# Experts' second layers by seven products, with combinations of tokens on GpSimd and the halves of images reordered

## Chip, cores and metric

The kernel runs on one core of a Trainium2 chip. The metric is the time of one execution on the device in microseconds (us), as the median of several runs. PE is the matmul engine, DVE the vector engine, ACT the scalar engine, POOL is GpSimd, SP issues most of the transfers. SBUF is the memory on the chip that holds the kernel's tiles; a bank is a tile of PSUM, into which PE writes its products.

## The reference

The program is two attention layers on 8 images of 256 channels and 32 x 32 pixels, with a mixture of experts at the end. The change concerns the experts alone. Every expert handles every token, and the gate weighs the results:

```python
def _L1_ffn_ref(x, Wr, br, W1, b1, g1, be1, m1, v1, W2, b2, g2, be2, m2, v2, Wo, bo):
    feat = jnp.mean(x, axis=0)                       # over all images
    w = jax.nn.softmax(feat @ Wr + br, axis=-1)      # the gates
    h = jnp.einsum('bfd,edh->bfeh', x, W1) + b1
    h = jax.nn.relu(_bn(h, g1, be1, m1, v1))
    h = jnp.einsum('bfeh,ehk->bfek', h, W2) + b2
    h = jax.nn.relu(_bn(h, g2, be2, m2, v2))
    y = jnp.einsum('bfeh,ehd->bfed', h, Wo) + bo
    return jnp.einsum('bfed,fe->bfd', y, w)
```

`feat` is a mean over all eight images, so no gate is known before the last image's attention has ended. First and second layers need no gate; the third does, since the kernel weighs its input and sums the experts on PE.

## The kernel before

The work comes in 128 units: 8 images, 2 halves of 512 pixels, 8 experts. Each unit has a first, a second and a third layer, each one product of a 256 x 256 weight with 256 x 512 data. First and third layers use **seven products** for eight (`products` and `sums`, Winograd's form of Strassen's scheme): the weights are combined once (`weights`), the tokens once per input (`combined`), and `sums` puts the result together on DVE. Second layers use eight plain products (`half`). Second layers that are done before the gates are known are stored in DRAM and fetched back later. `f` is a small model of the engines' times by which background work is placed; it emits the instructions.

```python
    def load(tile_i):
        b, half = divmod(tile_i, 2)
        f.finish(lambda: ended[0] > b)
        h = xs[tile_i] = T(work, [P, 2, 512], "hn", bufs=3)
        f.sp.dma_start(h, hn[b][:, :, half * 512 : half * 512 + 512])
...
    def bank():
        return T(psum, [P, 512], "bank", bufs=4)

    def half(dst, wt, e, src, s, c, m):

        ps = bank()
        for k in range(2):
            f.pe.matmul(ps, lhsT=wt[:, k, m * P : (m + 1) * P], rhs=src[:, k, :], start=k == 0, stop=k == 1)
        f.act.activation(dst[:, m, :], ps, AF.Relu, bias=col(c, e, m), scale=col(s, e, m))

    def where(i):
        tile_i, e = divmod(i, NE)
        b, half = divmod(tile_i, 2)
        return tile_i, e, b, slice(half * 512, half * 512 + 512)
...
    def blocks(w):

        return w[:, 0, :P], w[:, 1, :P], w[:, 1, P:]

    def weights(w, tag, pool):
        s = T(pool, [P, 4, P], tag)
        a11, a12, a22 = blocks(w)
        f.pool.tensor_tensor(s[:, 0, :], w[:, 0, P:], a22, ALU.add)
        f.pool.tensor_tensor(s[:, 1, :], s[:, 0, :], a11, ALU.subtract)
        f.pool.tensor_tensor(s[:, 2, :], a11, w[:, 0, P:], ALU.subtract)
        f.pool.tensor_tensor(s[:, 3, :], a12, s[:, 1, :], ALU.subtract)
        return s

    def combined(h, tag, pool=work):

        t = T(pool, [P, 4, C], tag, bufs=2)
        f.ve.tensor_tensor(t[:, 0:2, :], h[:, :, C:], h[:, 0, :].rearrange("p (n q) -> p n q", n=2), ALU.subtract)
        f.ve.tensor_tensor(t[:, 2, :], h[:, 1, C:], t[:, 0, :], ALU.subtract)
        f.ve.tensor_tensor(t[:, 3, :], h[:, 1, :C], t[:, 2, :], ALU.subtract)
        return t
...
    def products(banks, w, s, h, t, begin, end):

        a11, a12, a22 = blocks(w)
        for bank, place, lhs, rhs in (
            (1, 0, a11, h[:, 0, :C]),
            (0, 0, a12, h[:, 1, :C]),
            (0, 1, s[:, 1, :], t[:, 2, :]),
            (2, 0, s[:, 0, :], t[:, 0, :]),
            (2, 1, s[:, 2, :], t[:, 1, :]),
            (3, 0, s[:, 3, :], h[:, 1, C:]),
            (3, 1, a22, t[:, 3, :]),
        ):
            f.pe.matmul(
                banks[bank][:, place * C : place * C + C],
                lhsT=lhs,
                rhs=rhs,
                start=begin and (end or place == 0),
                stop=end and (begin or place == 1 or bank == 1),
            )

    def sums(banks):

        c = T(work, [P, 4, C], "c", bufs=2)
        u = T(work, [P, 2, C], "u", bufs=2)
        p26, p57, p34 = (banks[i].rearrange("p (u q) -> p u q", u=2) for i in (0, 2, 3))
        p1 = T(work, [P, 1, C], "p1c", bufs=2)
        f.act.activation(p1[:, 0, :], banks[1][:, :C], AF.Copy)
        f.ve.tensor_tensor(c[:, 0::2, :], p1.to_broadcast([P, 2, C]), p26, ALU.add)
        f.ve.tensor_tensor(u, c[:, 2:3, :].to_broadcast([P, 2, C]), p57, ALU.add)
        f.ve.tensor_tensor(c[:, 3, :], u[:, 1, :], p57[:, 0, :], ALU.add)
        f.ve.tensor_tensor(c[:, 1:3, :], u, p34, ALU.add)
        return c.rearrange("p (m n) q -> p m (n q)", m=2)

    def first7(i):
        tile_i, e, _, _ = where(i)
        if tile_i not in ts:
            ts[tile_i] = combined(xs[tile_i], "t1")
        h = h1s[i] = T(work, [P, 2, 512], "h1", bufs=2)
        banks = [bank() for _ in range(4)]
        products(banks, w1[e], s1[e], xs[tile_i], ts[tile_i], True, True)
        c = sums(banks)
        for m in range(2):
            f.act.activation(h[:, m, :], c[:, m, :], AF.Relu, bias=col(1, e, m), scale=col(0, e, m))
        loaded(i)
        if e == NE - 2 and tile_i + 1 in xs:
            ts[tile_i + 1] = combined(xs[tile_i + 1], "t1")

    def second(i, staged):
        _, e, _, _ = where(i)
        h, src = T(work, [P, 2, 512], "h2", bufs=5), h1s.pop(i)
        for m in range(2):
            half(h, w2[e], e, src, 2, 3, m)
            yield
        if staged:
            f.sp.dma_start(h2d[i], h)
        else:
            h2s[i] = h

    def fetch(i):
        if i not in h2s:
            h = h2s[i] = T(work, [P, 2, 512], "h2", bufs=5)
            f.sp.dma_start(h, h2d[i])
...
    f.step((PACE2, PACE2))
    while not gated and n2 < NSTAGED:
        ahead()
    f.finish(lambda: gated)
    early.close()
    wp3 = ctx.enter_context(tc.tile_pool(name="w3", bufs=1, side="right"))

    gb = T(wp3, [P, NE, HW], "gates")
    f.split(gb, *(512 * i for i in range(1, 2 * NE)))
    for part in range(2):
        sl = slice(part * 512, part * 512 + 512)
        for e in range(NE):
            f.sp.dma_start(gb[:, e, sl], gtd[e : e + 1, sl].to_broadcast([P, 512]))
    psum_y = ctx.enter_context(tc.tile_pool(name="psum_y", bufs=1, space=PSUM, side="right"))

    def weigh(i):
        _, e, _, sl = where(i)
        h = h2s[i]
        f.ve.tensor_tensor(h, h, gb[:, e : e + 1, sl].to_broadcast([P, 2, 512]), ALU.mult)
        h2s[i] = h, combined(h, "t3", wp3)

    def third(i):
        tile_i, e, b, sl = where(i)
        if e == 0:
            y = [T(psum_y, [P, 512], f"y{m}") for m in range(4)]
            t = T(work, [P, 2, 512], "t2")
            f.sp.dma_start(t, t2[b][:, :, sl])
            f.ve.tensor_tensor(t, t, gated[0][:, :, sl], ALU.add)
            ys[tile_i] = y, t
        y, t = ys[tile_i]
        products(y, wo[e], s3[e], *h2s.pop(i), e == 0, e == NE - 1)
        if e == NE - 1:
            f.ve.tensor_tensor(t, sums(y), t, ALU.add)
            f.sp.dma_start(out[b].rearrange("(k p) n -> p k n", p=P)[:, :, sl], t)
            ys.pop(tile_i)

    s3 = {}
    for i in range(NE):
        s3[i] = weights(wo[i], f"s3e{i}", wp3)

    def thirds(count):
        nonlocal n3
        for _ in range(count):
            if n3 < n2:
                if n3 + 2 < n2:
                    fetch(n3 + 2)
                if n3 + 1 < n2:
                    weigh(n3 + 1)
                third(n3)
                n3 += 1

    for i in range(2):
        ahead()
        fetch(i)
    weigh(0)
    while n3 < total:
        many = n2 > n3 + 2
        if n2 < n1 - 1 or n1 == total and n2 < total:
            halves = second(n2, n2 > n3 + 2)
            next(halves)
            thirds(1)
            for _ in halves:
                pass
            n2 += 1
            if many:
                thirds(1)
        else:
            thirds(1 + many)
        if n1 < total:
            first7(n1)
            n1 += 1
```

Of the kernel before, what the change touches and what calls it, by code (L numbers as in the profile page):

```python
# [10 lines left out]
AF = mybir.ActivationFunctionType  # L11
ALU = mybir.AluOpType
# [22 lines left out]
AHEAD = {"DVE": 4.0, "ACT": 2.0, "POOL": 1.0, "SP": 10.0}  # L35
NEAR = {"DVE": 1.5, "ACT": 2.0, "POOL": 1.0, "SP": 10.0}
BUFS = {"sm": 2, "sx": 1}
PACE2 = 8.0
NBOUND = 64
NSTAGED = 64  # L40
# [1947 lines left out]
def experts(tc, kit, nb, t2, hn, h2d, w1c, w2_d, wo_d, bnvec, bo_d, gate_d, wrc, consts8, gtd, out, f, outer, ended, early):  # L1988
# [8 lines left out]



    with ExitStack() as ctx:  # L2000
        l1, shared = outer
        wp = ctx.enter_context(tc.tile_pool(name="w2", bufs=1))
# [4 lines left out]
        xs = {}  # L2007

        def load(tile_i):
            b, half = divmod(tile_i, 2)  # L2010
            f.finish(lambda: ended[0] > b)
            h = xs[tile_i] = T(work, [P, 2, 512], "hn", bufs=3)
            f.sp.dma_start(h, hn[b][:, :, half * 512 : half * 512 + 512])

        w1, w2, wo = ([T(wp, [P, 2, C], f"{name}{e}") for e in range(NE)] for name in ("w1e", "w2e", "wo"))
# [73 lines left out]
        def col(what, e, m):  # L2089
            return bnvec[:, what * 2 * NE + 2 * e + m : what * 2 * NE + 2 * e + m + 1]  # L2090

        h1s, h2s, ys, ts = {}, {}, {}, {}

        def bank():
            return T(psum, [P, 512], "bank", bufs=4)
# [7 lines left out]

        def where(i):
            tile_i, e = divmod(i, NE)
            b, half = divmod(tile_i, 2)
            return tile_i, e, b, slice(half * 512, half * 512 + 512)

        def loaded(i):
# [5 lines left out]

        def first(i):
            tile_i, e, _, _ = where(i)
            h = h1s[i] = T(work, [P, 2, 512], "h1", bufs=2)
            for m in range(2):
                half(h, w1[e], e, xs[tile_i], 0, 1, m)  # L2120
            loaded(i)
# [11 lines left out]
            f.pool.tensor_tensor(s[:, 3, :], a12, s[:, 1, :], ALU.subtract)  # L2133
            return s

        def combined(h, tag, pool=work):

            t = T(pool, [P, 4, C], tag, bufs=2)
            f.ve.tensor_tensor(t[:, 0:2, :], h[:, :, C:], h[:, 0, :].rearrange("p (n q) -> p n q", n=2), ALU.subtract)
            f.ve.tensor_tensor(t[:, 2, :], h[:, 1, C:], t[:, 0, :], ALU.subtract)  # L2140
            f.ve.tensor_tensor(t[:, 3, :], h[:, 1, :C], t[:, 2, :], ALU.subtract)
            return t

        def products(banks, w, s, h, t, begin, end):
# [17 lines that stand above are left out]
                    stop=end and (begin or place == 1 or bank == 1),  # L2162
                )

        def sums(banks):

            c = T(work, [P, 4, C], "c", bufs=2)
            u = T(work, [P, 2, C], "u", bufs=2)
            p26, p57, p34 = (banks[i].rearrange("p (u q) -> p u q", u=2) for i in (0, 2, 3))
            p1 = T(work, [P, 1, C], "p1c", bufs=2)  # L2170
            f.act.activation(p1[:, 0, :], banks[1][:, :C], AF.Copy)
            f.ve.tensor_tensor(c[:, 0::2, :], p1.to_broadcast([P, 2, C]), p26, ALU.add)
            f.ve.tensor_tensor(u, c[:, 2:3, :].to_broadcast([P, 2, C]), p57, ALU.add)
            f.ve.tensor_tensor(c[:, 3, :], u[:, 1, :], p57[:, 0, :], ALU.add)
            f.ve.tensor_tensor(c[:, 1:3, :], u, p34, ALU.add)
            return c.rearrange("p (m n) q -> p m (n q)", m=2)

        def first7(i):
            tile_i, e, _, _ = where(i)
            if tile_i not in ts:  # L2180
                ts[tile_i] = combined(xs[tile_i], "t1")
            h = h1s[i] = T(work, [P, 2, 512], "h1", bufs=2)
            banks = [bank() for _ in range(4)]
            products(banks, w1[e], s1[e], xs[tile_i], ts[tile_i], True, True)
            c = sums(banks)
            for m in range(2):
                f.act.activation(h[:, m, :], c[:, m, :], AF.Relu, bias=col(1, e, m), scale=col(0, e, m))
            loaded(i)
            if e == NE - 2 and tile_i + 1 in xs:
                ts[tile_i + 1] = combined(xs[tile_i + 1], "t1")  # L2190

        def second(i, staged):
            _, e, _, _ = where(i)
            h, src = T(work, [P, 2, 512], "h2", bufs=5), h1s.pop(i)
            for m in range(2):
                half(h, w2[e], e, src, 2, 3, m)
                yield
            if staged:
                f.sp.dma_start(h2d[i], h)
            else:  # L2200
                h2s[i] = h

        def fetch(i):
            if i not in h2s:
                h = h2s[i] = T(work, [P, 2, 512], "h2", bufs=5)
                f.sp.dma_start(h, h2d[i])

        total = 2 * nb * NE
        f.spawn(gates(), 7)
        n1 = n2 = n3 = 0  # L2210
        s1 = {e: weights(w1[e], f"s1e{e}", wp) for e in range(NE)}

        def ahead():
            nonlocal n1, n2

            (first if n1 < 3 else first7)(n1)
            if n1 == 0:
                ts[0] = combined(xs[0], "t1")
            n1 += 1
            f.step((PACE2, PACE2))  # L2220
            if n1 > 1:
                for _ in second(n2, True):
                    pass
                n2 += 1
                f.step((PACE2, PACE2))

        f.step((PACE2, PACE2))
        while not gated and n2 < NSTAGED:
            ahead()
        f.finish(lambda: gated)  # L2230
        early.close()
        wp3 = ctx.enter_context(tc.tile_pool(name="w3", bufs=1, side="right"))

        gb = T(wp3, [P, NE, HW], "gates")
        f.split(gb, *(512 * i for i in range(1, 2 * NE)))
        for part in range(2):
            sl = slice(part * 512, part * 512 + 512)
            for e in range(NE):
                f.sp.dma_start(gb[:, e, sl], gtd[e : e + 1, sl].to_broadcast([P, 512]))
        psum_y = ctx.enter_context(tc.tile_pool(name="psum_y", bufs=1, space=PSUM, side="right"))  # L2240

        def weigh(i):
            _, e, _, sl = where(i)
            h = h2s[i]
            f.ve.tensor_tensor(h, h, gb[:, e : e + 1, sl].to_broadcast([P, 2, 512]), ALU.mult)
            h2s[i] = h, combined(h, "t3", wp3)

        def third(i):
            tile_i, e, b, sl = where(i)
            if e == 0:  # L2250
                y = [T(psum_y, [P, 512], f"y{m}") for m in range(4)]
                t = T(work, [P, 2, 512], "t2")
                f.sp.dma_start(t, t2[b][:, :, sl])
                f.ve.tensor_tensor(t, t, gated[0][:, :, sl], ALU.add)
                ys[tile_i] = y, t
            y, t = ys[tile_i]
            products(y, wo[e], s3[e], *h2s.pop(i), e == 0, e == NE - 1)
            if e == NE - 1:
                f.ve.tensor_tensor(t, sums(y), t, ALU.add)
                f.sp.dma_start(out[b].rearrange("(k p) n -> p k n", p=P)[:, :, sl], t)  # L2260
                ys.pop(tile_i)

        s3 = {}
        for i in range(NE):
            s3[i] = weights(wo[i], f"s3e{i}", wp3)

        def thirds(count):
            nonlocal n3
            for _ in range(count):
                if n3 < n2:  # L2270
                    if n3 + 2 < n2:
                        fetch(n3 + 2)
                    if n3 + 1 < n2:
                        weigh(n3 + 1)
                    third(n3)
                    n3 += 1

        for i in range(2):
            ahead()
            fetch(i)  # L2280
        weigh(0)
        while n3 < total:
            many = n2 > n3 + 2
            if n2 < n1 - 1 or n1 == total and n2 < total:
                halves = second(n2, n2 > n3 + 2)
                next(halves)
                thirds(1)
                for _ in halves:
                    pass
                n2 += 1  # L2290
                if many:
                    thirds(1)
            else:
                thirds(1 + many)
            if n1 < total:
                first7(n1)
                n1 += 1


@with_exitstack  # L2300
# [179 lines left out]
```

## Time and profile before

| | before |
|---|---|
| median of the runs, us | 3362.33 (3358.39 to 3362.58) |
| busy PE / DVE / ACT / POOL, us | 3175.6 / 2311.2 / 1688.4 / 511.1 |
| first matmul of the experts | 2002.02 us, after 8.55 us of waiting |
| first third layer | 2289.97 us, after 10.97 us of waiting |
| last two matmul records of the third layers start | 3347.21 us |

Lines of the timeline give start, duration, engine, instruction and what ended an idle time before it in brackets; durations of matmuls overlap in the pipeline, so lengths here are differences of starts. The transfers issued by SP at the moment the gates are known:

```profile
2267.42 11.79 SPq L668 DMA_DIRECT2D gates<-gtd  x16
...
2280.27 3.27 SPq L668 DMA_DIRECT2D h<-h  x5
```

Sixteen broadcasts of gates occupy the queue until 2279.2 us. The stored second layer that the first third layer needs is fetched behind them. The second view is the group of the weighing on DVE (busy time, mean ns of one, idle time before it):

```profile
L668 DVE TENSOR_TENSOR h<-h,gates 128x1024 f32<-128x1024 f32 x127 | 154.7, 1218 | 7.1 <-ACT h L668 7.1
```

### The profile page before, as it was taken

Reading aid. Unit: us, or ns where it says so; the run is one execution under the profiler, and the core shown is the slowest. Engines: PE = TensorE matmul, PEld = TensorE weight load, DVE = VectorE, ACT = ScalarE, POOL = GpSimd, SP = SyncE. Lnnn points to the kernel's source line nnn. Section 1 sums busy time; section 2 is a strip of 40 time slices with the busy share of each in tenths; the row PEclk is TensorE's granted clock in tenths of the full one; section 3 lists DMA queues with packets and bytes.
Section 4 is the critical chain, followed back from the end, with each engine's and each line's share of the span. In section 5 each row is a group of like instructions: output and inputs, shape, how many; then the busy total and the mean of one; then the engine's idle time right before and its main releaser. Section 6 shows DMA issues by size and latency. Waiting matters only on the chain.

```text
span 3365.0 us, 40262 instructions
## 1 busy us (share of the span) xinstructions
PE 3175.6 (94%) x15352; PEld 1801.8 (54%) x15352; DVE 2311.2 (69%) x3972; ACT 1688.4 (50%) x2225; POOL 511.1 (15%) x644
## 2 busy tenths in 40 slices
PE   8687899899899999899899989998999999999997
PEld 4332244344345345345344346766777777777775
DVE  5687787886886886887874446346776666666665
ACT  4476676576576666666666533342223333333332
POOL 2211414213214114214211120010000000000000
PEclk9798999999999999999999999999999999999999
DMA  2357646656646655556556565125441100000000
GB/s 74 83 120 166 130 98 155 130 103 150 131 102 142 141 134 122 121 137 126 115 124 139 117 184 184 51 93 189 145 155 65 36 19 19 19 19 19 19 13 20
DMA packets 106363, 345.88 MB, mean 103 GB/s; under 512 B 13025, under 2 KB 38377, under 8 KB 82929
## 3 DMA queue, kind: packets, MB, share of 16 engines
q0 software_dynamic: 28608, 179.85, 27.8%
q1 hardware_dynamic: 74192, 161.40, 13.9%
q8 instruction: 123, 2.02, 0.2%
q10 hardware_dynamic: 3360, 1.97, 0.2%
q14 instruction: 80, 0.65, 0.1%
HBM read 104.59 MB, written 73.44 MB: 53 GB/s over the span
## 4 chain that ended last, share of the span: by engine, by line
PE 64%; DMA 2%; ACT 2%; issue 2%; DVE 1%; POOL 1%; SPq 0%; ACTq 0%; POOLq 0%; DVEq 0%
PE bank L668 23%; PE sm L668 13%; PE y L668 12%; PE sc L668 6%; PE sx L668 6%; PE pv L668 5%; ACT pt L668 2%; DMA pt<-pt 1%; DMA hn<-hn 0%; DMA feat<-hn 0%; POOL rstd L668 0%; DVE rec L668 0%; DMA gates<-gtd 0%; DMA w1e<-w1c 0%; POOL pt L668 0%
## 5 line engine op out<-in xcount | busy, mean ns | idle before, releaser
L668 ACT ACTIVATE pt<-sc 128x2048 f32<-128x2048 f32 (+1 forms) x384 | 719.9, 1875 | 326.1 <-PE sc L668 278.4
L668 DVE SCALAR_TENSOR_TENSOR acc<-p,vec,acc 128x225 f32<-128x225 f32 (+7 forms) x928 | 527.8, 576 | 29.4 <-ACT acc L668 4.9
L668 PE MATMUL sc<-q,kn 32*128 32x512 f32 (+1 forms) x3072 | 445.8, 650 | 95.8 <-ACT pt L668 94.4
L668 DVE TENSOR_TENSOR pt<-pt,pt 128x1024 f32<-128x1024 f32 x320 | 387.4, 1254 | 141.0 <-DMA pt<-pt 136.1
L668 PE MATMUL bank<-h,w2e 128*128 128x512 f32 x1024 | 480.1, 595 | 0.0
L668 PE MATMUL pv<-pt,vt 128*32 128x512 f32 (+1 forms) x3072 | 418.0, 617 | 0.0
L668 ACT ACTIVATE h<-bank,bnvec 128x512 f32<-128x512 f32 x262 | 201.3, 769 | 385.7 <-PE bank L668 374.0
L668 ACT ACTIVATE h<-c,bnvec 128x512 f32<-128x512 f32 x250 | 189.9, 807 | 385.7 <-DVE c L668 385.7
L668 DVE TENSOR_TENSOR c<-p1c,bank 128x512 f32<-128x512 f32 x125 | 85.9, 687 | 350.9 <-PE bank L668 349.9
L668 POOL DMA_DIRECT2D pt<-pt x192 | 173.9, 907 | 779.0 <-ACT pt L668 628.4
L668 PEld LDWEIGHTS bank<-h,w2e 128*128 128x128 f32 x1024 | 195.2, 191 | 149.8 <-issue 134.9
L668 PEld LDWEIGHTS sc<-q,kn 32*128 32x128 f32 (+1 forms) x3072 | 116.3, 178 | 284.8 <-ACT pt L668 185.5
L668 PEld LDWEIGHTS pv<-pt,vt 128*32 128x32 f32 (+1 forms) x3072 | 60.7, 108 | 301.8 <-issue 290.1
L668 POOL TENSOR_TENSOR rstd<-rstd,mhalf 128x4 f32<-128x4 f32 (+2 forms) x88 | 107.9, 1227 | 675.6 <-DVE rstd L668 616.4
L668 PE MATMUL y<-t,s3e 128*128 128x256 f32 x768 | 188.0, 381 | 0.0
L668 PE MATMUL bank<-t,s1e 128*128 128x256 f32 x750 | 183.2, 380 | 0.2 <-ACT h L668 0.2
L668 PE MATMUL sm<-y,t 128*128 128x256 f32 x752 | 180.9, 385 | 0.0
L668 DVE TENSOR_TENSOR h<-h,gates 128x1024 f32<-128x1024 f32 x128 | 156.0, 1218 | 19.3 <-issue 12.2
L668 PEld LDWEIGHTS sm<-y,t 128*128 128x128 f32 x752 | 137.8, 190 | 56.5 <-issue 35.1
L668 ACT ACTIVATE p<-sm 128x512 f32<-128x512 f32 (+1 forms) x151 | 88.4, 585 | 145.2 <-PE sm L668 122.0
L668 PEld LDWEIGHTS y<-t,s3e 128*128 128x128 f32 x768 | 146.8, 191 | 20.2
L668 PEld LDWEIGHTS bank<-t,s1e 128*128 128x128 f32 x750 | 143.1, 191 | 20.2 <-ACT h L668 0.6
(303 smaller groups left out, 4689.4 us busy)
## 6 DMA issues: line engine op xcount, KB each, us to landing
pt<-pt POOLq DMA_DIRECT2D x160, 1024.0 KB, 7.4
h<-h SPq DMA_DIRECT2D x88, 512.0 KB, 3.8
xi<-in_x_dram SPq DMA_DIRECT2D x16, 512.0 KB, 6.7
t<-t SPq DMA_DIRECT2D x8, 1024.0 KB, 9.3
res<-t SPq DMA_DIRECT2D x32, 256.0 KB, 4.1
t<-res SPq DMA_DIRECT2D x32, 256.0 KB, 4.9
hn<-res SPq DMA_DIRECT2D x32, 256.0 KB, 2.9
hn<-hn SPq DMA_DIRECT2D x16, 512.0 KB, 5.5
```

Source lines behind the costliest of these rows:

```text
L668: ins = fn(*args, **kwargs)
```

## The change

Intent: less matmul work after the gates. PE is the bound there, GpSimd is idle, and PE also waits once at the gates. The change has these parts:

- second layers go by seven products too, once the gates are known (`strassen = bool(s3)`): weights' sums `s2` and tokens' combinations `tm` on GpSimd;
- most combinations for third layers move to GpSimd as well (`weighed(f.pool)`), except that in the first passes (rounds of the loop at the end of the cut), where two third layers go with one second (`many`), one of the two stays on DVE;
- the two activations of a seven-product layer are held back until the next layer's copy (`late`, `flush`);
- tiles are in the order of halves: the first half of all eight images, then the second. Eight gate rows are held for sixteen, and each is replaced when its half is done;
- at the gates, three stored layers are fetched before the broadcasts, and a first layer stands before the first third layer;
- the start of the experts may take up to eight steps of background work for one;
- the residual of a half image is fetched and added nearer to its end.

The diff, cut to its core:

```diff
-            b, half = divmod(tile_i, 2)
+            half, b = divmod(tile_i, nb)
...
-        def combined(h, tag, pool=work):
+        def combined(h, tag, pool=work, eng=f.pool):
...
+        def layer7(e, w, s, src, t, first, tag, bufs, then):
+            banks = [bank() for _ in range(4)]
+            products(banks, w[e], s[e], src, t, True, True)
+            h = sums(banks, tag, bufs)
+
+            def relu():
+                for m in range(2):
+                    f.act.activation(h[:, m, :], h[:, m, :], AF.Relu, bias=col(first + 1, e, m), scale=col(first, e, m))
+                then(h)
+
+            late.append(relu)
 
         def first7(i):
...
+            strassen = bool(s3)
+            if strassen and e not in s2:
+                s2[e] = weights(w2[e], f"s2e{e}", wp3)
+
+            def then(h):
+                h1s[i] = h
+                if strassen:
+                    tms[i] = combined(h, "tm", wp3)
+
+            layer7(e, w1, s1, xs[tile_i], ts[tile_i], 0, "h1", 3, then)
...
         def second(i, staged):
...
+            if i in tms:
+                layer7(e, w2, s2, src, tms.pop(i), 2, "h2", 6, then)
             else:
-                h2s[i] = h
+                h = T(work, [P, 2, 512], "h2", bufs=6)
+                for m in range(2):
+                    half(h, w2[e], e, src, 2, 3, m)
+                then(h)
...
-        f.step((PACE2, PACE2))
+        for _ in range(NE):
+            f.step((PACE2, PACE2))
+            if max(f.ready[a.name] for a in (w1[0], xs[0])) <= f.now["PE"]:
+                break
...
         f.finish(lambda: gated)
+        for i in range(AHEAD3):
+            fetch(i)
...
-        gb = T(wp3, [P, NE, HW], "gates")
-        for part in range(2):
...
+        def spread(e, sl):
+            gb[e] = T(wp3, [P, 1, 512], f"gate{e}")
+            f.sp.dma_start(gb[e][:, 0, :], gtd[e : e + 1, sl].to_broadcast([P, 512]))
+
+        for e in range(NE):
+            spread(e, slice(0, 512))
...
+        def weighed(eng):
+            if n3 + AHEAD3 < n2:
+                fetch(n3 + AHEAD3)
+            if n3 + 1 < n2:
+                weigh(n3 + 1, eng)
...
         while n3 < total:
             many = n2 > n3 + 2
             if n2 < n1 - 1 or n1 == total and n2 < total:
-                halves = second(n2, n2 > n3 + 2)
...
+                second(n2, many)
                 n2 += 1
                 if many:
-                    thirds(1)
-            else:
-                thirds(1 + many)
+                    weighed(f.pool)
+                    thirds()
+            weighed(f.ve if many else f.pool)
             if n1 < total:
                 first7(n1)
                 n1 += 1
+            thirds()
```

## The prediction

> **What bounds the kernel now.** I read the page's engine shares and slices first, then the sums by stretch, then the timeline of the last stretch, then the waits around the moment the gates become known. The first lines to read are these:
>
> ```profile
> PE 3175.6 (94%) x15352; PEld 1801.8 (54%) x15352; DVE 2311.2 (69%) x3972; ACT 1688.4 (50%) x2225; POOL 511.1 (15%) x644
> PE   8687899899899999899899989998999999999997
> DVE  5687787886886886887874446346776666666665
> POOL 2211414213214114214211120010000000000000
> ```
>
> PE is busy 94% of the span, and from slice 28 on it never drops. The experts' part after the gates is slices 28 to 40. There GpSimd (POOL) does nothing and DVE is about 60 to 70% busy. The sums by stretch (PE, PEld, DVE, ACT, POOL) say it sharply:
>
> ```profile
> 2002.00:2280.00 278.00, 273.08 (x1026) 190.74 (x1026) 128.47 (x236) 103.92 (x175) 40.78 (x77) 0.98 0.38 130
> 2290.00:2450.00 160.00, 160.00 (x635) 122.44 (x636) 115.58 (x175) 41.35 (x64) 0.00 (x0) 0.98 0.43 150
> 2570.00:3348.00 778.00, 777.80 (x2956) 561.17 (x2954) 477.58 (x745) 266.35 (x417) 0.00 (x0) 1.00 0.06 19
> ```
>
> From 2290 to 3348 us PE has no gap. Only two things shorten that stretch: fewer matmul columns, or nothing. The timeline there shows what one unit (one expert on one half image) costs; second layer = bank<-h,w2e, first layer = bank<-hn,..., third layer = y:
>
> ```profile
> 3001.74 1.88 PE L668 MATMUL bank<-h,w2e 128*128 128x512 f32 x4
> 3003.46 1.03 PE L668 MATMUL bank<-hn,w1e 128*128 128x256 f32 x4
> ...
> 3006.48 1.88 PE L668 MATMUL bank<-h,w2e 128*128 128x512 f32 x4
> 3008.20 1.03 PE L668 MATMUL y<-h,wo 128*128 128x256 f32 x4
> ...
> 3011.22 1.88 PE L668 MATMUL bank<-h,w2e 128*128 128x512 f32 x4
> ```
>
> Durations overlap in this pipeline, so I use starts. Half a second layer takes 3003.46 - 3001.74 = 1.72 us, a whole one 3.44 us (8 matmul records of 0.43). A seven-product layer takes 3006.48 - 3003.46 = 3.02 us (14 records of 0.216). A unit is 3.44 + 3.02 + 3.02 = 9.48 us.
>
> The one large hole of PE in the experts' part is at the gates:
>
> ```profile
> 2275.40 3.60 PE L668 MATMUL bank<-h,w2e 128*128 128x512 f32 x8
> 2289.97 2.08 PE L668 MATMUL y<-h,wo 128*128 128x256 f32 x4 [10.97 <-DVE h L668]
> 2291.84 2.77 PE L668 MATMUL y<-t,s3e 128*128 128x256 f32 x6
> ```
>
> PE waits 10.97 us for the first weighing on DVE, and the ten records after it take 4.4 us of starts instead of 2.2: the clock has to come back. A smaller hole, 8.55 us, lies at 2002 us, where the first hn and weights are loaded.
>
> **What the Trainium skill says.** (1) "TensorE: Matmul & The Clock Gate", Part 1: an idle array drops to half clock and needs some microseconds of activity to return. The trace agrees: 0.52 us per 256-column record after the hole against 0.26 by its record mean, both including pipeline time, or 2.08 against 1.03 for the same four. (2) "GPSIMD Engine Reference", section 3: two-input elementwise work is about half as fast on GpSimd. Here 128x512 with two SBUF inputs takes 1.32 us on POOL (pool<-xi) and 0.69 us on DVE (t<-h); 128x256 takes 0.78 against 0.42. (3) "SBUF — State Buffer", section "Who interferes with whom": a DVE instruction with two SBUF inputs and a GpSimd instruction that reads SBUF block each other for a whole instruction; with at most one SBUF input DVE is free of it. The trace agrees: the shared stretch below has two DVE additions of 1.22 us each taking 3.33 us and two POOL additions, otherwise 0.95 us each, taking 2.95 us.
>
> ```profile
> 1285.05 3.33 DVE L668 TENSOR_TENSOR pt<-pt,pt 128x1024 f32<-128x1024 f32 x2
> 1287.37 2.95 POOL L668 TENSOR_TENSOR pool<-pool,xi 128x320 f32<-128x320 f32 x2
> ```
>
> **The change, part by part.**
>
> *Second layers on PE.* Of 1024 w2e records (8 per unit, 128 units), 194 start before 2285 us, so about 24 second layers are done when the loop starts. The unit whose first layer came just before also has no combination ready. That leaves 128 - 25 = 103 layers to switch: 103 x (3.44 - 3.02) = 43 us less on PE.
>
> *The hole at the gates.* Before, sixteen gate broadcasts of 256 KB (4 MB) take the queue from 2267.4 to 2279.2 us and the fetch of the first stored h2 stands behind them. Now three fetches go first, only eight broadcasts (2 MB) follow, and a first layer is put ahead of the first third layer. I expect 11 us of waiting and 2 us of slow clock gone: 13 us. The start at 2002 us may now run background work while the load lands; but a background matmul is only taken if its data is already there, so I count 2 of 8.55 us.
>
> *The order of halves* makes the gates of one half enough for eight images. About 22 units are done before the gates, which needs images 0 to 4 only, all ended by then. I count no time for it.
>
> *DVE.* Each switched layer adds four sums: 0.69 + 0.69 + 0.42 + 0.68 = 2.48 us, so 103 x 2.48 = +255 us. About 104 of the 128 third-layer combinations (0.69 + 2 x 0.42 = 1.54 us) go to POOL: -160 us. Net about +95 us, to some 2405 us.
>
> *POOL.* A combination costs 1.32 + 2 x 0.78 = 2.9 us; 103 for the second layer and 104 for the third give 600 us, plus 8 x 1.85 us for the weights' sums (four of 0.46 us per expert). POOL goes from 511 to about 1125 us.
>
> *ACT.* Two activations (1.54 us) become a copy (0.37) and two activations (1.6): +0.4 us x 103 = 41 us, beside the rest.
>
> **Does that fit under PE?** About 20 loop passes come first in which two third layers are done per second layer (44 of the h<-h transfers' 88 are stores, 24 of them before the loop). PE needs 4 x 3.02 = 12.1 us a pass. DVE has two sets of sums (5.0), two weighings (2.4), one combination (1.5), and on average 1.4 for the y sums, residuals and t1: 10.4 us. POOL has 5.8 us, and in the first eight passes up to 5.5 more for weights. The two-SBUF-input part of DVE (about 4.8 us) plus POOL is 10.6 us, and up to 16 in the first passes: it must be run one after the other while the sums also wait their turn on DVE. I expect here 0.9 us of PE waiting per pass, 18 us, and 8 more while the weights are made.
> In the other 84 passes PE needs 9.07 us, DVE 5.0 + 1.2 + 0.8 = 7.0, POOL 5.8. Second and first layer now stand next to each other on PE and share four banks: from the trace the first DVE sum starts 1.56 us after a layer's first matmul and the last ends 4.1 us after, while the next layer needs the last bank at 3.02 + 2.2 = 5.2 us. So banks are free in time unless DVE is late by over about 0.9 us. It is late once per eight passes, when the y sums (2.5) and the residual (1.2) come on top: about 0.8 us x 11 = 8 us. The last two units add the longer POOL combination to the end: 2 us.
>
> Sum: 3362 - 43 - 13 - 2 + 18 + 8 + 8 + 2 = 3340 us. The losses are my weakest terms, taken at the pessimistic end of a hand-drawn order of instructions; the deferred activations and the split of combinations between engines look tuned to avoid them. I halve them, 36 to about 20, and predict **3325 us**.
>
> **Rivals.** (A) *Nothing is lost*: PE stays at 100%, 3362 - 58 = 3304 us. For it: DVE and POOL sums both lie below PE in every pass. Against it: the lock above, and one set of four banks. (B) *DVE with the shared port becomes the bound* in the first 20 passes, and banks come free late in the others: 36 to 55 us lost, so 3340 to 3360 us, the change nearly cancelled. For it: the 3.33 us pair above, and 16 us of shared work in the first passes. Against it: after eight passes it falls below PE's time. (C) *The staged part before the gates gets slower*, because activations are held back behind the next layer's copy, or because loading an image that has not ended stalls the stream: +5 to 20 us. For it: each held-back activation has only some 0.4 us to spare. Against it: images 0 to 4 end long before.
>
> **Range and chances.** A gives the low end with a few us for the start, 3298; B without C gives 3355. Faster by 2% means below 3295 us, 67 us less: it needs all of A and the whole start, 6%. Slower by 2% means above 3430, for which B and C together do not suffice: 2%. Within 2%: 92%.
>
> **What would show each step.** PE records: w2e at 512 columns falls to about 200, and the new 256-column second-layer records start 0.216 us apart. The hole of 10.97 us is below 3 us. DVE is near 2405 us busy and POOL near 1125. Lost time shows as idle PE before bank or y records released by DVE sums or POOL combinations, most of it in the first 250 us after the gates and then once per eight units. POOL and DVE combinations longer than 1.32 and 0.69 us show the lock. I am wrong if PE is idle over 40 us after the gates, or if the part before them changes by over 15 us.

## The result, and the profile after

The median is **3332.22 us** (four runs, 3328.18 to 3334.62) against 3362.45 us for the kernel before in the same rounds (3358.39 to 3368.05). The ratio is 0.9908, with a 95% interval of 0.9889 to 0.9926: within 2%. Outputs are correct.

Busy time and slices of the page after:

```profile
PE 3137.4 (94%) x15970; PEld 1912.8 (57%) x15970; DVE 2472.4 (74%) x4069; ACT 1734.4 (52%) x2328; POOL 1227.3 (37%) x1300
...
PE   8687899999999999899899999999999999999997
...
DVE  5687788786887886886884555446998787787776
...
POOL 2211413213213214213211112006666776777775
```

PE has 38 us less, DVE 161 more, POOL 716 more. POOL now works from slice 28 to the end. The dip of PE's row at the gates (slice 28 before) is gone. The timeline of PE there, and SP's queue:

```profile
2273.62 3.60 PE L669 MATMUL bank<-h,w2e 128*128 128x512 f32 x8
2277.05 1.03 PE L669 MATMUL bank<-hn,w1e 128*128 128x256 f32 x4
...
2280.08 1.03 PE L669 MATMUL y<-h,wo 128*128 128x256 f32 x4
```

```profile
2265.15 2.56 SPq L669 DMA_DIRECT2D h<-h  x4
2267.81 6.37 SPq L669 DMA_DIRECT2D gate<-gtd  x8
```

No bracket: the third layer follows the first layer without a wait, and at 1.03 us for four records the clock is at full speed (2.08 before). The steady loop, 700 us later:

```profile
2974.64 1.03 PE L669 MATMUL bank<-h,w2e 128*128 128x256 f32 x4
...
2977.66 1.03 PE L669 MATMUL bank<-hn,w1e 128*128 128x256 f32 x4
...
2980.69 1.03 PE L669 MATMUL y<-h,wo 128*128 128x256 f32 x4
...
2983.71 1.03 PE L669 MATMUL bank<-h,w2e 128*128 128x256 f32 x4
```

Each layer takes 3.02 us, the unit 9.07 us instead of 9.48. So the matmuls shrank as planned. What came in exchange stands in the sums by stretch (stretch, its length, busy PE, PEld, DVE, ACT, POOL with their instructions, clock, DMA share, GB/s):

```profile
2280.20:2555.00 274.80, 261.89 (x1187) 223.80 (x1186) 246.78 (x311) 78.57 (x130) 183.51 (x174) 1.00 0.42 149
...
2555.00:3293.00 738.00, 735.58 (x3397) 644.36 (x3396) 578.98 (x819) 303.45 (x496) 526.61 (x485) 1.00 0.08 25
```

In the first 275 us after the gates PE is idle for 12.9 us, and a busy PE is not yet a full one. Counted by records (1187, of which 8 are 512 columns wide and count double, at 0.216 us) the work is 258.1 us, so 16.7 us are lost there. In the 738 us of the steady loop, 3397 x 0.216 = 733.7 us: 4.3 lost. Who was waited for in the two stretches (total us, times, longest):

```profile
PE y L669 <- POOL t L669: 8.6, 7, 1.8
PE bank L669 <- DVE h L669: 4.1, 5, 1.1
...
PE bank L669 <- DVE h L669: 2.4, 10, 0.3
```

Before, PE waited for nothing after its one hole at the gates. One pass of the first stretch shows how these waits arise:

```profile
2392.17 1.30 POOL L669 TENSOR_TENSOR tm<-h 128x512 f32<-128x512 f32 x1 [6.86 <-ACT h L669]
...
2392.84 3.39 DVE L669 TENSOR_TENSOR h<-h,gate 128x1024 f32<-128x1024 f32 x2
...
2393.55 3.27 POOL L669 TENSOR_TENSOR tm<-h,tm 128x256 f32<-128x256 f32 x2
...
2396.78 1.74 POOL L669 TENSOR_TENSOR t<-h 128x512 f32<-128x512 f32 x1
...
2398.60 1.66 POOL L669 TENSOR_TENSOR t<-h,t 128x256 f32<-128x256 f32 x2
...
2399.44 1.56 PE L669 MATMUL y<-t,s3e 128*128 128x256 f32 x6 [0.99 <-POOL t L669]
```

Two weighings on DVE (1.22 us each before) take 3.39 us, two GpSimd subtractions (0.78 us each by the prediction's row) take 3.27, and they lie in the same 4 us. GpSimd gets to the third layer's combination `t` late, and PE waits 0.99 us for it. Over the whole part after the gates, DVE's and POOL's groups:

```profile
L669 DVE TENSOR_TENSOR h<-h,gate 128x1024 f32<-128x1024 f32 x126 | 206.6, 1649 | 2.5 <-DMA h<-h 2.1 <-ACT h L669 0.5
```

```profile
L669 POOL TENSOR_TENSOR tm<-h,tm 128x256 f32<-128x256 f32 x206 | 247.6, 1202 | 16.1
```

The weighing went from 1218 to 1649 ns, the subtraction from 0.78 to 1.20 us. The sums on DVE, with one input in SBUF and one in PSUM, ran beside the same GpSimd and kept their 0.69 us (688 ns before):

```profile
L669 DVE TENSOR_TENSOR u<-h,bank 128x512 f32<-128x512 f32 x206 | 141.6, 687 | 21.7
```

On DVE only the instructions with two SBUF inputs got longer in this part. That is what the Trainium skill's "SBUF — State Buffer", "Who interferes with whom", leads one to expect of a two-input DVE instruction beside a GpSimd one that reads SBUF. Whether it is the cause is tested below.

**The balance of the profiled runs.** The span went from 3365.0 to 3332.1 us, 32.9 less. I split it at the start of the first third layer (2289.97 and 2280.08) and at the start of the last two records of the last one (3347.21 and 3313.95).

| stretch | before | after | difference |
|---|---|---|---|
| start to the first third layer | 2289.97 | 2280.08 | -9.9 |
| first third layer to the last | 1057.2 | 1033.9 | -23.4 |
| rest | 17.8 | 18.1 | +0.3 |

The first row is the hole at the gates (-11.0) and a start of the experts that came 1.1 us later (2003.16 for 2002.02; over the runs below, experiment 10 left out, this start lies between 1996.6 and 2003.7 us, so 1.1 us says nothing of the change). From that start, without the hole, both kernels take 277 us, though the changed one does one first layer more in it; why this layer is free there I did not settle. The second row is 103 switched layers x 0.41 us of PE = -42.2, that one first layer done earlier = -3.0, the slow clock after the hole = -1.9, and PE's waiting = **+24.5**: -22.6 together, with 0.8 left over. The 24.5 us come from experiment 1, which has no waiting: its 1051.6 us for this stretch less 42.2 is 1009.4 us of work, and the changed kernel took 1033.9. By place it is 16.7 in the first 275 us, 4.3 in the steady loop and 2.1 in the last two units (waits of 1.32 and 0.45 us on POOL with the pipeline's restart); the remaining 1.4 are within the accuracy of the count. The first row varies: over all profiled runs of the changed kernel and its variants without a hole the first third layer starts between 2273.6 and 2280.1 us, though the program before it is the same (but for the order of halves in experiment 5; experiment 10 is left out). Where small differences matter I therefore compare the second row and not the time.

### The profile page after: what moved, and what is told of

Same layout as the page of the kernel before. It is cut to its first block, busy times and chain, and to the rows that moved or that the text cites. A ratio compares the mean times of both kernels' runs of the same rounds, so it can differ in the third digit from the quotient of the medians.

```text
span 3332.1 us, 42942 instructions
## 1 busy us (share of the span) xinstructions
PE 3137.4 (94%) x15970; PEld 1912.8 (57%) x15970; DVE 2472.4 (74%) x4069; ACT 1734.4 (52%) x2328; POOL 1227.3 (37%) x1300
## 4 chain that ended last, share of the span: by engine, by line
PE 57%; DVE 5%; issue 3%; ACT 3%; POOL 3%; DMA 2%; SPq 0%; DVEq 0%; POOLq 0%; ACTq 0%
PE bank L669 18%; PE sm L669 13%; PE y L669 8%; PE sc L669 6%; PE sx L669 6%; PE pv L669 5%; DVE h L669 2%; ACT pt L669 2%; POOL tm L669 1%; DVE u L669 1%; DMA pt<-pt 1%; ACT h L669 1%; POOL t L669 1%; DVE t L669 1%; DVE c L669 1%
## 5 line engine op out<-in xcount | busy, mean ns | idle before, releaser
L669 ACT ACTIVATE p1c<-bank 128x256 f32<-128x256 f32 x228 | 87.2, 383 | 576.4 <-PE bank L669 576.1
L669 ACT ACTIVATE h<-h,bnvec 128x512 f32<-128x512 f32 x456 | 345.0, 805 | 50.7 <-DVE h L669 43.7
L669 DVE TENSOR_TENSOR h<-p1c,bank 128x512 f32<-128x512 f32 x228 | 155.2, 681 | 194.7 <-PE bank L669 191.2
L669 POOL TENSOR_TENSOR tm<-h,tm 128x256 f32<-128x256 f32 x206 | 247.6, 1202 | 16.1
L669 DVE TENSOR_TENSOR h<-u,bank 128x256 f32<-128x256 f32 x456 | 232.1, 550 | 7.9
L669 POOL TENSOR_TENSOR tm<-h 128x512 f32<-128x512 f32 x103 | 133.9, 1300 | 245.2 <-ACT h L669 241.2
L669 DVE TENSOR_TENSOR h<-h,gate 128x1024 f32<-128x1024 f32 x128 | 209.1, 1642 | 2.5 <-DMA h<-h 2.1
L669 PE MATMUL bank<-h,w2e 128*128 128x256 f32 (+1 forms) x612 | 198.8, 453 | 4.1 <-DVE h L669 4.1
L669 POOL TENSOR_TENSOR t<-h,t 128x256 f32<-128x256 f32 x210 | 177.4, 845 | 16.5
L669 DVE TENSOR_TENSOR u<-h,bank 128x512 f32<-128x512 f32 x228 | 156.7, 687 | 24.0
```

The lines of the kernel that those rows point to most:

```text
L669: ins = fn(*args, **kwargs)
```

## The experiments

My theory: the products give their 42 us and the hole its 13; PE gives 24.5 us back, and it does so because DVE and GpSimd hold each other up over SBUF while both work for the same PE. Rivals: that GpSimd is simply too slow or too late; that the weights' sums made in the first passes are to blame; that the new order of halves brought the gain. All edits below are against the changed kernel. "Waiting" is computed as above: the stretch from the first to the last third layer, less the work, which is 1051.6 us minus 0.41 us per switched layer. It rests on one profiled execution of each kernel; experiments 1 and 5, with the same work, agree in it (1051.62 us both). It counts more than the idle time that the profile shows, since PE is not at once at its full pace after a wait (the six records after the 0.99 us wait above took 1.56 us, six without a wait 1.46).

### 1. Full second layers

```diff
-            strassen = bool(s3)
+            strassen = False
```

> Second layers back to eight full-width records everywhere, all else of the change kept. Theory (43 us of matmul time bought, some 24 us of it given back as PE waiting after the gates): PE work rises by 103 x 0.42 = 43 us, DVE loses 255 us and GpSimd 300 us of work, so the waiting after the gates falls from 24 to about 5 us; time about 3332 + 43 - 19 = 3356 us, and against the kernel before only the hole at the gates is gained. Rival (the products bought nothing, the gain is all in the order of transfers at the gates): time stays at 3330 to 3335 us.

Measured: 3348.08 us (3343.41 to 3351.52), ratio 0.9967 (0.9946 to 0.9988). The weighing took 1220 ns again. PE over the experts' part after the gates:

```profile
2275.00:3326.00 1051.00, 1051.00 (x4049) 768.95 (x4048) 511.39 (x730) 343.00 (x532) 306.62 (x335) 1.00 0.16 56
```

PE is busy for 1051.00 of 1051.00 us: all the waiting belongs to the seven-product second layers, although 105 of the 128 third layers' combinations are still on POOL. (Some 5 us of waiting were expected to stay; so the run was 8 us faster than expected.) The switch of the second layers is worth 1051.6 - 1033.9 = 17.7 us net, of 42.2 gross.

### 2. Gates before the fetches

Sixteen broadcasts (each of the eight sent twice) ahead of the three fetches:

```diff
-        for i in range(AHEAD3):
-            fetch(i)
...
-        for e in range(NE):
-            spread(e, slice(0, 512))
+        for _ in range(2):
+            for e in range(NE):
+                spread(e, slice(0, 512))
+        for i in range(AHEAD3):
+            fetch(i)
```

> Sixteen gate broadcasts (each of the eight sent twice) ahead of the three fetches of stored second layers, as the kernel before had it; all else of the change kept. Theory (the 11 us hole was the queue: 4 MB of broadcasts in front of the fetch): a PE gap of 5 to 10 us in front of the first third layer, less than before because one first layer now stands ahead of it, and time 3338 to 3343 us. Rival (the hole closed because a first layer now stands ahead, or because GpSimd makes the weights one expert at a time): no gap over 2 us, time 3330 to 3335 us.

Measured: 3340.75 us (3338.46 to 3344.44), ratio 0.9947 (0.9928 to 0.9965), so about 8 us slower than the changed kernel. SP's queue and PE at the gates:

```profile
2260.30 11.90 SPq L669 DMA_DIRECT2D gate<-gtd  x16
```

```profile
2281.83 2.08 PE L669 MATMUL y<-h,wo 128*128 128x256 f32 x4 [6.93 <-DVE h L669]
```

The hole comes back with its slow clock. It is 6.93 us and not 10.97, and the first layer that the change put ahead of the third one would account for 3.02 of those 4 us. So the order of the transfers is shown to matter; that the first layer in front does is argued from its length, not tested.

### 3. Combinations for second layers made only twice (wrong result)

```diff
-                    tms[i] = combined(h, "tm", wp3)
+                    if len(kept) < 2:
+                        kept.append(combined(h, "tm", wp3))
+                    tms[i] = kept[i % len(kept)]
```

> Wrong result on purpose: GpSimd makes the combination of second-layer inputs only twice and every second layer uses one of the two; PE, DVE and ACT run the same instructions, GpSimd loses about 101 x 3 instructions. Theory (the waiting after the gates comes from GpSimd and DVE blocking each other and from GpSimd's own queue): DVE's weighing falls from a mean of 1649 ns to 1220 to 1350, PE waiting after the gates from 24 us to under 8, time about 3315 us. Rival (the waiting is DVE's own sums and the four shared banks): weighing as it may be, waiting stays above 18 us and time at 3326 to 3334 us.

Measured: 3311.38 us (3306.03 to 3313.51), ratio 0.985 (0.9831 to 0.9869), waiting 7.0 us; the weighing took 1233 ns. All seven-product matmuls and all sums on DVE are still there. So the 101 combinations that GpSimd no longer made cost 17.5 of the 24.5 us, and DVE's added sums alone do not. This does not yet say how: by occupying GpSimd's queue or by locking DVE.

### 4. All weights' sums before the first weighing

```diff
         for i in range(2):
             ahead()
+        for i in range(NE):
+            s3[i] = weights(wo[i], f"s3e{i}", wp3)
+            e = (n1 + i) % NE
+            s2[e] = weights(w2[e], f"s2e{e}", wp3)
         weigh(0)
```

> The sums of weights for second and third layers (16 x 4 GpSimd instructions of 0.46 us) all issued at once when the gates are known, when GpSimd is idle, instead of one expert at a time inside the first eight passes. Theory (17 of the 24 us of waiting lie in the first 275 us after the gates, about half of it because weights and combinations together overload GpSimd): 6 us less, 3326 us, and the waits of y for GpSimd in the first 100 us gone. Rival (that waiting is the lock and DVE, not the weights): 3330 to 3335 us.

Measured: 3333.57 us (3331.1 to 3339.18), ratio 0.9925 (0.9904 to 0.9945), waiting 27.4 us. No gain. In the first 100 us from the first third layer on, POOL was busy for 66.6 us in place of 79.0, and yet PE was idle for 6.0 us, in the changed kernel for 5.7; in the next 100 us, idle for 3.7 us in both. So the weights' sums are not what the first passes wait for, and of the prediction's 8 us for them at most some 2 (5.7 - 3.7) can have been there.

### 5. The old order of halves

With seven products in the second layers the old order could not be built: if the gates of both halves are held at once, the pool `w3` needs 80 KB per partition where 66.9 KB were left (no run shows it). So the order was tested with full second layers, against experiment 1: the two changes of `where` and `load` undone, sixteen gate tiles, and

```diff
-            half, b = divmod(tile_i, nb)
+            b, half = divmod(tile_i, 2)
...
-            strassen = bool(s3)
+            strassen = False
```

> Old order of halves (both halves of an image in turn, sixteen gate tiles, the second eight sent while the first half image is weighed), with second layers full as in the run before named full second, because with seven products it does not fit: the last pool then asks for 80 KB per partition and 66.9 KB are left. Theory (the order buys room, not time): within 6 us of the full-second run, 3343 to 3354 us, no gap over 2 us at the gates. Rival (the order itself closes part of the hole): a gap of 4 us or more before the first third layers, 3352 us or more.

Measured: 3349.3 us (3347.47 to 3353.22), ratio 0.9966 (0.9948 to 0.9983), against 0.9967 for experiment 1, no gap at the gates, and the same 1051.62 us from the first to the last third layer. The order buys no time. What it buys is room: with all gates held, the seven products do not fit in the old order.

### 6. Seven products only when the stored layers are used up

```diff
-            strassen = bool(s3)
+            strassen = bool(s3) and n2 - n3 <= 4
```

> Seven products only for second layers that are met once third layers no longer come two per pass: some 20 fewer switched layers. Theory (GpSimd and DVE are overloaded only in those first passes; 17 of 24 us of waiting lie there): PE work up by 20 x 0.41 = 8 us, waiting down by 14 to 16 us, time about 6 us under the changed kernel, 3325 us, and waiting after the gates 8 to 10 us. Rival (waiting does not depend on the combinations of the second layer in those passes, or only moves): 3332 to 3340 us.

Measured: 3318.65 us (3316.47 to 3322.05), ratio 0.9873 (0.9855 to 0.989). Of the 103 layers 83 are switched, which costs PE 20 x 0.41 = 8.2 us, and waiting falls from 24.5 to 6.6 us. From the first to the last third layer that is 1024.2 us against 1033.9, 9.7 us less; the rest of the 13.6 us between the medians lies before that stretch, which began earlier here (2273.75 us), and is not owed to this edit as far as I can tell. In the first 20 passes, where two third layers go with one second, the seven products cost more than they give. The weighing still takes 1.50 us on average here: the lengthening is there in the later passes too, but costs PE little. Those passes leave DVE more room: in the changed kernel it was busy for 579 of 738 us in them, for 247 of 275 in the first ones.

### 7. The same, and the last combinations on DVE

```diff
-            strassen = bool(s3)
+            strassen = bool(s3) and n2 - n3 <= 4
...
-            weighed(f.ve if many else f.pool)
+            weighed(f.ve if many or n1 == total else f.pool)
```

> The same, and the combinations of the last four or so third layers on DVE, where nothing else is left for it. Theory (at the end the chain runs through GpSimd's 2.9 us and PE waits 1.3 and 0.45 us for it): 1.5 to 2 us under the run before, some 3323 us, no wait of y for GpSimd in the last 30 us. Rival (DVE is as late): no difference.

Measured: **3316.10 us** (3315.6 to 3316.43), ratio 0.9863 (0.9846 to 0.9879), correct; the fastest correct kernel here, 45 us below the one before in the same rounds (3361.56). Its busy times and its first stretch after the gates:

```profile
PE 3137.5 (95%) x15850; PEld 1890.4 (57%) x15850; DVE 2388.4 (72%) x3998; ACT 1727.6 (52%) x2308; POOL 1127.5 (34%) x1231
```

```profile
2281.00:2555.00 274.00, 274.00 (x1112) 211.09 (x1111) 166.95 (x242) 78.13 (x121) 92.57 (x105) 1.00 0.43 146
```

PE has no gap in the stretch that had 12.9 us of idle time, and no third layer waits for POOL any more. Waiting is 4.5 us, nearly all of it in the steady loop, where PE still waits for its banks nine times for DVE's sums (2.2 us idle); the weighing takes 1.50 us. The 2 us against experiment 6 show in the profile; the two ratios' intervals overlap.

### 8. All combinations for third layers on DVE

```diff
-                    weighed(f.pool)
+                    weighed(f.ve)
...
-            weighed(f.ve if many else f.pool)
+            weighed(f.ve)
```

> All third-layer combinations on DVE, only those of second layers on GpSimd. Theory (DVE is then 8.5 us of 9.07 in a steady pass and about 12 of 12.1 in the early ones, with the lock on top, so it becomes the bound): waits of y for GpSimd gone, but waits of banks for DVE sums rise to 40 us or more, 3345 to 3365 us; the change needs both sets of combinations on GpSimd. Rival (GpSimd's own queue is what costs, DVE has room): waiting falls under 15 us, 3320 us.

Measured: 3355.12 us (3351.83 to 3359.08), ratio 0.9979 (0.996 to 0.9998), waiting 53 us. PE's main wait after the gates:

```profile
PE bank L669 <- DVE h L669: 17.9, 50, 1.1
```

Now PE waits for its banks, 50 times, because DVE gets to the sums late (and 24 times, 9.0 us, for ACT's copy in `sums`). So GpSimd's share of the combinations is needed: less lock is not better if DVE takes the work itself.

### 9. Three memsets in place of a combination (wrong result)

```diff
-                    tms[i] = combined(h, "tm", wp3)
+                    tms[i] = T(wp3, [P, 4, C], "tm", bufs=2)
+                    for _ in range(3):
+                        f.pool.memset(tms[i], 0.0)
```

> Wrong result on purpose: each of GpSimd's second-layer combinations is replaced by three memsets of the whole tile, which keep GpSimd's queue occupied (if each takes 0.5 us or more, 1.5 us or more in place of 2.9) but read nothing of SBUF. Against the run that made them only twice (waiting after the gates 7 us) this tells the lock from the queue. Theory (DVE's two-input instructions and GpSimd's reading ones exclude each other): DVE's weighing stays near 1230 ns, waiting near 7 us, time about 3315 us. Rival (GpSimd's queue comes late for the third layers whatever runs in it): waiting stays above 15 us, 3325 us or more.

Measured: 3311.04 us (3308.93 to 3313.43), ratio 0.9851 (0.9836 to 0.9866), waiting 5.8 us. One memset took 951 ns, three 2.85 us, as long as an undisturbed combination (2.9 us by the prediction). The weighing took 1230 ns. GpSimd was occupied as long, but only wrote, and the waiting was as small as in experiment 3. One doubt stays: these memsets did not wait for the activation that makes `h`, as the real combination does.

### 10. The start of the experts filled by force

Experiment 7, and ten pieces of background work before the first expert:

```diff
             f.step((PACE2, PACE2))
             if max(f.ready[a.name] for a in (w1[0], xs[0])) <= f.now["PE"]:
                 break
+        for _ in range(10):
+            f.credit = [1.0, 1.0]
+            near = [t for t in f.threads if f.possible(t[1])]
+            f.resume(next((t for t in f.threads if t[1][0] is None and t[1][1]()), None) or min(near, key=f.start))
```

> The best version so far (products late, tail on DVE) with ten pieces of the remaining attention forced in front of the first expert, while its weights and image are loaded; the change's own loop there runs eight times and takes no matmul beyond the first step, because the recorded times say that the data is not ready. Theory (the 9 us gap at 2002 us is a wait that other work can stand in): gap 0 to 3 us, time 5 to 9 us under the run before, about 3309 us. Rival (the forced pieces wait for DVE and ACT themselves, and their gaps come in its place): 3314 to 3320 us.

Measured: 3332.88 us (3327.74 to 3337.7), ratio 0.9913 (0.9899 to 0.9926), 17 us slower than experiment 7. PE's main waits around the start:

```profile
PE sm L669 <- DVE res L669: 9.4, 1, 9.4
PE sm L669 <- POOL diag L669: 8.3, 1, 8.3
```

The wait for the first load fell from 9.1 to 2.9 us, and two new ones took its place. What was pulled forward had inputs that were not there; PE stands in order behind it. And most of the 17 us lie after the gates: two first and two second layers fewer were done before them (318 and 176 matmul records before the first third layer for 346 and 192), and the stretch from the first to the last third layer took 1034.4 us for 1022.1, without more idle PE than in experiment 7. This idea of mine failed.

### 11. Memsets that wait like the combination (wrong result)

```diff
-                    tms[i] = combined(h, "tm", wp3)
+                    f.pool.memset(h, 0.0)
+                    tms[i] = T(wp3, [P, 4, C], "tm", bufs=2)
+                    for _ in range(2):
+                        f.pool.memset(tms[i], 0.0)
```

> Wrong result on purpose: as the run with memsets, but the first of the three memsets writes the second layer's input itself, so that GpSimd waits for ACT before it as the real combination does; 2.85 us of queue, the same wait, and no reading of SBUF. The run before removed the lock and that wait together. Theory (the lock alone): weighing near 1230 ns, waiting after the gates 6 to 9 us, 3309 to 3316 us. Rival (the combination's wait for ACT at the head of GpSimd's queue makes the third layer's combination late): waiting back above 15 us, 3322 us or more.

Measured: 3312.30 us (3309.45 to 3314.81), ratio 0.9855 (0.9838 to 0.9872), waiting 6.9 us (3292.24 - 2275.99 = 1016.25 us, less 1009.4). The first and the last two records of the third layers, then the groups of POOL and DVE:

```profile
2275.99 1.03 PE L669 MATMUL y<-h,wo 128*128 128x256 f32 x4
...
3292.24 0.59 PE L669 MATMUL y<-t,wo 128*128 128x256 f32 x2
```

```profile
L669 POOL MEMSET h<- 128x1024 f32 x103 | 98.0, 951 | 331.9 <-ACT h L669 331.8
```

```profile
L669 DVE TENSOR_TENSOR h<-h,gate 128x1024 f32<-128x1024 f32 x125 | 152.6, 1230 | 2.4 <-DMA h<-h 2.0 <-ACT h L669 0.5
```

GpSimd waits for ACT here as in the changed kernel and is occupied as long as an undisturbed combination takes. Only its reading of SBUF is gone, and with it 24.5 - 6.9 = 17.6 us of waiting. So the blocking of the two engines over their reads of SBUF, the "lock" of these texts, is the cause of 17.6 of the 24.5 us; GpSimd's undisturbed pace and its wait for ACT are not. In the steady loop the waiting is gone altogether: PE is busy for 720.00 of the 720.00 us from 2551 on. Two things stay open. The lock lengthens both sides, DVE's weighing (1.23 to 1.65 us) and GpSimd's combination (2.9 to 1.30 + 2 x 1.20 = 3.70 us), and which of the two makes PE late was not separated. And the 6.9 us that are left (2.1 of them in the last two units) were not taken apart; third layers' combinations on GpSimd still read SBUF here. (Zeros in `h` and `tm` change no matmul's length: a seven-product second layer here starts at 2973.09 us and the next layer at 2976.11, 3.02 us later.)

## Why the prediction was right, and where it was not

The prediction's 3325 us lay 7 us below the measured 3332.2, inside its range. By its own steps:

- **PE, 43 us:** right. The `bank<-h,w2e` records fell from 1024 to 612 = 25 x 8 + 103 x 4 (a switched layer has four of that name), of which 200 are still 512 columns wide; 103 x 0.41 = 42.2 us. (The prediction's 194 early records counted two twice, at the edges of its windows: it is 192, 24 layers, as it says.)
- **The hole, 13 us:** right. 10.97 us of waiting and 1.9 of slow clock are gone, and experiment 2 brings both back. The slow clock came with the hole each time: 2.08 us for four records after it, 1.03 without it.
- **The start, 2 us:** wrong. PE waited 9.09 us instead of 8.55. The loop that may take background work put no further matmul there: 10258 PE records come before the experts' first one in both kernels. Experiment 10 agrees with the reason that the prediction gives against it, that other data is not there yet.
- **The order of halves, no time:** right, by experiment 5. That it makes the room for the seven products was not foreseen.
- **DVE and POOL:** the size failed. DVE was predicted to have 95 us more and had 161, POOL 614 and had 716. The counts of instructions were right; the durations were taken from undisturbed rows. The weighing's extra 126 x 0.43 = 54 us is most of DVE's difference; 43 subtractions of the combinations left on DVE, 0.82 for 0.42 us each (17 us), and other two-input instructions are the rest (records that overlap count once in the busy time, so the terms do not add up exactly). On POOL, 206 x (1.20 - 0.78) = 87 us, and 210 of the third layers' at 0.845 (14 us), are its difference. These longer durations count as busy time. ACT, with 41 us more expected, had 46.
- **The losses, 20 us:** the mechanism was right, and so was the place. Worked out were 18 + 8 in the first passes, 8 in the steady loop and 2 at the end, 36 in all, then halved by judgement. Measured: 16.7, 4.3, 2.1, with 24.5 in all. In the steady loop PE waited for its banks 10 times, about once per eight units, as foreseen, at half the cost. The 8 us for weights' sums is the term that was hardly there (experiment 4); without it the worked sum would have been 28, a little nearer to 24.5 than the halved 20. That 20 came as near as it did is partly luck: the halving made up for a term that was wrong and one that was twice too large. Halving a sum as a whole hid which of its terms was doubtful.

Of the remaining 7 us, 4.5 are more waiting and 2 the start that gained nothing; the rest is below what one start of the experts differs from the next. Rival A (nothing lost, 3304 us) is refuted by the waits; rival B had the right mechanism, lock and banks, at about half the size it was given (24.5 for 36 to 55 us), but PE waited more for GpSimd's combinations (8.6 us in the first stretch) than for DVE's sums (4.1); rival C (a slower part before the gates) did not appear, 277 us in both kernels.

Where did the expected gain go? Of 42.2 us that PE saves, 24.5 came back as waits that had not existed before, two thirds of it in the first 275 us. There two third layers go with each second layer: DVE has both weighings, and GpSimd the second layer's combination and one of the third layers', so that the two are in each other's way most. Leaving the second layers whole in that stretch keeps 34 us of the 42 (83 x 0.41) and takes 17.9 of the 24.5 us of waiting away (experiment 6).

## What to carry to other kernels

Work given to an idle GpSimd is not free where DVE runs instructions with two SBUF inputs beside it: price both at their blocked duration, and look at the stretch in which both have most to do for the same consumer. A saving on the bound engine can be switched on only where the helpers have room, here after the stored layers were used up, which gave 9.7 us more in that part than switching it on everywhere. Memsets in place of reading instructions, with the same waits, separate a lock from a slow engine in one run. And a longer instruction is not yet a loss: with 1.50 us for the weighing, PE waited 4.5 us in experiment 7; with 1.65 us and no room in the first passes, 24.5.

## What the Trainium skill lacked or had wrong

- "SBUF — State Buffer": its rule agrees with the runs here, also in that a GpSimd instruction that only writes does not hold up a two-input DVE one (1230 ns for the weighing beside memsets, 1220 without the combinations, 1649 beside them). It lacks a size for a mixed stream: here the mean rose by 35% on DVE and 54% on GpSimd (0.78 to 1.20 us), and PE lost 17.6 us by it.
- "GPSIMD Engine Reference": it lists memset without a rate of its own. Here a 128x1024 float32 memset took 0.95 us.
- No page says that one float32 matmul shows as two records in the trace (14 records for seven products; 0.216 us each at 256 columns, 0.43 at 512). It matters for every count of instructions above.
